# Two layers of directional convolution scans: contiguous map rows, column state in small tiles, lanes 64 steps apart, chains turned over in groups of eight rows

## The chip, the core and the metric

The kernel runs on one core of one Trainium2 chip. The metric is the device time of one launch in microseconds (us). The core has five engines that run side by side and wait for each other by semaphores: PE (TensorE, matrix products), DVE (VectorE), ACT (ScalarE), POOL (GpSimd) and SP (SyncE), which here issues nearly all DMAs between HBM and SBUF. Every engine works through its own instructions strictly in order.

## What is computed

Input `x` is float32 [32 batches, 48 channels, 64 rows h, 128 columns w]. Two layers follow each other, each `x = x + scan(groupnorm(x))`, where the group norm has 16 groups per batch and the scan is four recurrences, each started from the result of the one before:

```python
nxt = inp + conv1d(carry, w, b)        # 5 taps, 48 x 48 channels, across the other axis
D = scan(down_w, rows 0..63)           # each row from the row above, conv along w
U = scan(down_w, rows of D, bottom up) # conv along w
R = scan(right_w, columns of U)        # each column from the one to its left, conv along h
L = scan(left_w, columns of R, right to left)
```

So a layer is 63 + 63 dependent row steps and 127 + 127 dependent column steps, and nothing of one batch's step can start before its previous step has ended. The parallelism is over batches.

## The kernel before

Channels of even and odd positions along the convolved axis lie side by side on the partitions (0 to 47 and 64 to 111, the `SIDES`; P = 112), so one step (`step`) is three accumulated 112 x 112 products into one PSUM tile (with the pair of positions before, the pair itself, the pair after), and one DVE instruction `scalar_tensor_tensor` (below: the update, L180) that adds PSUM, bias and the input and writes the new state. Each float32 product shows as two PE records, so a step is six records.

Four batches make a chain (G = 4), so a row step (`d`, `u` in the names) works on 4 x 64 = 256 columns of the moving operand and a column step (`r`, `l`) on 4 x 32 = 128. Two chains are in flight, one per lane. `run_lane` is a Python generator that yields after each step, and the driver calls the two lanes in turn: step n of lane 0, step n of lane 1, and so on. Both lanes are always at the same step of the same scan. A list scheduler then sets the final order of each engine.

The map of a lane lies in SBUF as [batch][pair of w][r][pair of h], that is `[P, G, WP, 2, HP]`. A column `col(v)` is 32 adjacent words per batch; a row `row(h)` is 64 words that lie 64 words (256 bytes) apart. The down scan runs in place on rows; the up scan writes its state to small contiguous tiles `carry` (two per lane), from which `place` (two ACT copies per step, L188) puts each row where the right and left scans read it; these two run in place on columns.

Between two scans stands a chain change. Whole batches move: `load_x` brings one batch in two DMAs of 768 KB, `add_scan` adds the map to it (POOL, L106), `store_x` writes it to `mid` (the layer 0 result in HBM) or `out`, `stats` takes its norm (8 `bn_stats` on DVE, a small matmul, a chain of one-column instructions), and `normalize` writes it into the map (half on ACT L152, half on POOL L159). Each lane has NX = 2 tiles for this. A chain goes through both layers before the next one starts, so there are 4 pairs of chains x 2 layers = 8 rounds.

## Time and profile before

| | us |
|---|---|
| three runs | 8436.22, 8440.92, 8441.28 (median 8440.92) |
| span of the profiled execution | 8440.7 |
| PE, DVE, ACT, POOL busy | 6745.4, 3721.4, 1902.0, 1264.6 |
| DMA by SP | 251.68 MB |

The span, from the first to the last instruction, is within 1 us of the median run, so rows of the profile can be set against the time directly. Busy times overlap and are not shares of a sum. PE's busy time contains products that take longer than their number of columns asks for, so it has to be read by stage.

### The profile page before, as it was taken

The page shows a single profiled execution, that of the slowest core. Times are in us where ns is not written, and L with a number is a line of the kernel's source. Part 1 is how long each engine was busy: PE and PEld are TensorE (multiplying, and loading weights), DVE is VectorE, ACT ScalarE, POOL GpSimd, SP SyncE. Part 2 cuts the span into 40 slices and gives each one's busy share as a digit, 9 for nine tenths or more (in the row PEclk, how much of TensorE's full clock was granted, in tenths as well). Part 3 has the DMA queues.
Part 4 walks back from the last instruction along what each step waited for, and adds up shares of the span by engine and source line. Part 5 has one row for each costly group of instructions (what it writes and reads, how often), then busy time and mean ns, then how long its engine had stood idle before and what let it go on. Part 6 is the DMA issues. An engine that isn't in the chain of part 4 may idle for free. (4 is left out here: it accounts for less than half of the span.)

```text
span 8440.7 us, 85243 instructions
## 1 busy us (share of the span) xinstructions
PE 6745.4 (80%) x36736; PEld 5026.5 (60%) x36736; DVE 3721.4 (44%) x7235; ACT 1902.0 (23%) x2241; POOL 1264.6 (15%) x199
## 2 busy tenths in 40 slices
PE   4999559994499955999449995599944999559993
PEld 2479524894247952489424795248942479524893
DVE  5345533553334553355333455335532345533552
ACT  3070110700207011070020701107012070110700
POOL 4000330003300033000330003300043000330004
PEclk9999779997699977999769997799976999779997
DMA  9000240005700024000570002400057000340005
GB/s 94 0 1 1 44 76 0 1 1 74 105 0 1 1 41 79 0 1 1 75 105 0 1 1 46 74 0 1 1 75 105 0 1 1 46 74 0 1 1 90
DMA packets 497403, 258.09 MB, mean 31 GB/s; under 512 B 5392, under 2 KB 496912, under 8 KB 497024
## 3 DMA queue, kind: packets, MB, share of 16 engines
q1 hardware_dynamic: 496640, 251.68, 20.7%
q8 instruction: 287, 4.70, 0.2%
q10 hardware_dynamic: 384, 0.96, 0.0%
q14 instruction: 92, 0.75, 0.0%
HBM read 151.95 MB, written 100.66 MB: 30 GB/s over the span
## 5 line engine op out<-in xcount | busy, mean ns | idle before, releaser
L106 POOL TENSOR_TENSOR x<-x,map 112x4096 f32<-112x4096 f32 x64 | 694.3, 10866 | 6611.4 <-issue 3290.5
L123 PE MATMUL ps_stat_x<-mv_x,mask_sb 112*112 112x1 f32 x64 | 16.4, 326 | 728.1 <-DVE mv_x L121 722.2
L188 ACT COPY map<-last 48x256 f32<-48x256 f32 x32 | 21.9, 683 | 2469.5 <-DVE last L180 2469.2
L123 PEld LDWEIGHTS ps_stat_x<-mv_x,mask_sb 112*112 112x112 f32 x64 | 14.9, 286 | 731.8 <-DVE mv_x L121 724.8
L135 ACT ACTIVATE std_m<-var_m 112x1 f32<-112x1 f32 x32 | 6.5, 203 | 1850.4 <-DVE var_m L132 1850.3
L123 PE MATMUL ps_stat_m<-mv_m,mask_sb 112*112 112x1 f32 x64 | 16.4, 326 | 473.8 <-DVE mv_m L121 448.6
L119 DVE BATCH_NORM_STATS2 st_x<-x 112x6 f32<-112x512 f32 x256 | 155.6, 679 | 513.9 <-DMA x<-in_x 513.7
L135 ACT ACTIVATE std_x<-var_x 112x1 f32<-112x1 f32 x32 | 6.5, 203 | 1615.1 <-DVE var_x L132 1615.1
L159 POOL TENSOR_SCALAR map<-x,scale_x,offset_x 48x2048 f32<-48x2048 f32 x64 | 277.8, 4341 | 346.3 <-DVE offset_x L145 340.3
L119 DVE BATCH_NORM_STATS2 st_m<-x 112x6 f32<-112x512 f32 x256 | 160.5, 679 | 340.7 <-POOL x L106 340.7
L159 POOL TENSOR_SCALAR map<-x,scale_m,offset_m 48x2048 f32<-48x2048 f32 x64 | 271.6, 4244 | 195.4 <-DVE offset_m L145 171.3
L123 PEld LDWEIGHTS ps_stat_m<-mv_m,mask_sb 112*112 112x112 f32 x64 | 14.9, 286 | 477.7 <-DVE mv_m L121 450.7
L152 ACT ACTIVATE map<-x,offset_x,scale_x 48x2048 f32<-48x2048 f32 x64 | 279.3, 4364 | 44.9 <-DVE offset_x L145 41.3
L152 ACT ACTIVATE map<-x,offset_m,scale_m 48x2048 f32<-48x2048 f32 x64 | 273.1, 4268 | 51.6 <-DVE offset_m L145 34.1
L130 PE MATMUL ps_stat_m<-sq_m,mask_sb 112*112 112x1 f32 x64 | 16.5, 328 | 151.9 <-DVE sq_m L129 151.9
L180 DVE SCALAR_TENSOR_TENSOR map<-ps_1L1d,b_sb,map 112x256 f32<-112x256 f32 x62 | 75.3, 1215 | 123.7 <-PE ps_1L1d L177 117.9
L180 DVE SCALAR_TENSOR_TENSOR map<-ps_3L1d,b_sb,map 112x256 f32<-112x256 f32 x62 | 75.5, 1217 | 123.1 <-PE ps_3L1d L177 118.0
L180 DVE SCALAR_TENSOR_TENSOR map<-ps_7L0d,b_sb,map 112x256 f32<-112x256 f32 x62 | 76.3, 1231 | 121.2 <-PE ps_7L0d L177 115.6
L180 DVE SCALAR_TENSOR_TENSOR map<-ps_7L1d,b_sb,map 112x256 f32<-112x256 f32 x62 | 75.5, 1217 | 123.0 <-PE ps_7L1d L177 117.9
L180 DVE SCALAR_TENSOR_TENSOR map<-ps_5L1d,b_sb,map 112x256 f32<-112x256 f32 x62 | 75.4, 1216 | 123.0 <-PE ps_5L1d L177 117.9
L180 DVE SCALAR_TENSOR_TENSOR map<-ps_3L0d,b_sb,map 112x256 f32<-112x256 f32 x62 | 76.4, 1232 | 120.7 <-PE ps_3L0d L177 115.4
L180 DVE SCALAR_TENSOR_TENSOR map<-ps_5L0d,b_sb,map 112x256 f32<-112x256 f32 x62 | 76.3, 1231 | 120.6 <-PE ps_5L0d L177 115.5
(617 smaller groups left out, 19622.9 us busy)
## 6 DMA issues: line engine op xcount, KB each, us to landing
x<-in_x SPq DMA_DIRECT2D x128, 768.0 KB, 16.3
mid<-x SPq DMA_DIRECT2D x64, 768.0 KB, 12.1
x<-mid SPq DMA_DIRECT2D x64, 768.0 KB, 16.0
out<-x SPq DMA_DIRECT2D x64, 768.0 KB, 12.6
w_sb<-in_w ACTq DMA_DIRECT2D x1, 882.0 KB, 12.2
mask_sb<-in_mask ACTq DMA_DIRECT2D x1, 49.0 KB, 1.9
b_sb<-in_b ACTq DMA_DIRECT2D x1, 2.6 KB, 5.4
```

What stands on the lines that cost most here:

```text
L106: nc.gpsimd.tensor_tensor(xt, xt, maps[lane][:, j].rearrange("c p r q -> c q (p r)"), ALU.add)
L119: nc.vector.bn_stats(st[:, s, :], flat[:, bass.ts(s, SEG)])
L123: nc.tensor.matmul(ps[:, 0:1], mask_sb, mv[:, 0:1], start=True, stop=True)
L130: nc.tensor.matmul(ps[:, 1:2], mask_sb, sq, start=True, stop=True)
L135: nc.scalar.activation(std, var, AF.Sqrt)
L152: nc.scalar.activation(maps[lane][SIDES[0], j, :, hs, :], view[hsl, :, 0, :], AF.Identity, bias=offset[hsl], scale=scale[hsl],)
L159: nc.gpsimd.tensor_scalar(maps[lane][SIDES[1], j, :, hs, :], view[hsl, :, 1, :], scale[hsl], offset[hsl], ALU.mult, ALU.add,)
L180: nc.vector.scalar_tensor_tensor(dst, ps, b_sb[:, layer, way : way + 1], inp, ALU.add, ALU.add)
L188: nc.scalar.copy(maps[lane][SIDES[hs], :, :, ws, q], carry[SIDES[ws]])
```

## The change

What it does, by parts:

- **Map layout.** The map becomes [batch][pair of h][r][pair of w], `[P, G, HP, 2, WP]`. Now `row(h)` is 64 adjacent words per batch, and `col(v)` is 32 words that lie 128 words (512 bytes) apart.
- **Column state.** The right and left scans no longer run in place. Each step writes a small contiguous tile `cur` (six per lane), the next step's products read that tile, and a POOL `tensor_copy` puts it into the map.
- **Lanes 64 steps apart.** Lane 0 starts 64 steps ahead of lane 1 (OFFSET). A lane also walks all its layer 0 chains first and then all its layer 1 chains.
- **Turn-over in groups.** The chain change is cut into NG = 8 groups of four row pairs (eight rows) of all four batches. Six tiles (`ring`) are shared by both lanes. For each group `turn_over` adds the old chain's map to its `x` rows (`turn_rows`, four POOL adds of 112 x 512), stores them, takes `bn_stats` for the next layer, and normalizes the new chain's rows into the same map rows (`normalize_rows`, 16 instructions of 48 x 256, on ACT, for the first group half on DVE). Groups 0 and 1 are turned over before the new down scan starts and group 2 ahead of its first step, one further group every eight steps. Each group takes eight load DMAs for the old rows, eight for the new, eight stores, of 96 KB each.
- **Statistics of x** come from a separate pass over `x` (`batch_stats`, `plan_stats`), spread over steps of the chain before by `spare()`; scales and offsets are kept for all chains.

```diff
-        cpool.tile([P, G, WP, 2, HP], F32, tag=f"map{i}", name=f"map{i}")
+        cpool.tile([P, G, HP, 2, WP], F32, tag=f"map{i}", name=f"map{i}")
...
+    def load_rows(src: bass.AP, chain: int, g: int) -> bass.AP:
+        t = free.pop(0)
+        for j in range(G):
+            for side in range(2):
+                nc.sync.dma_start(t[SIDES[side], j], rows(src, chain, g, j, side))
+        return t
...
+    def turn_rows(lane: int, layer: int, chain: int, g: int, t: bass.AP, st):
+        dst = out if layer else mid
+        for j in range(G):
+            mine = t[:, j].rearrange("c q (p r) -> c q r p", r=2)
+            nc.gpsimd.tensor_tensor(
+                mine, mine, maps[lane][:, j, g * GH : (g + 1) * GH], ALU.add
+            )
+        store_rows(dst, chain, g, t)
+        if st is not None:
+            for j in range(G):
+                nc.vector.bn_stats(st[:, j, g, :], t[:, j].rearrange("c q w -> c (q w)"))
+    def normalize_rows(lane: int, layer: int, chain: int, g: int, t: bass.AP, split: bool):
...
+                    if split and ws:
+                        nc.vector.tensor_scalar(dst, src, s, o, ALU.mult, ALU.add)
+                    else:
+                        nc.scalar.activation(dst, src, AF.Identity, bias=o, scale=s)
...
-            nc.scalar.copy(maps[lane][SIDES[hs], :, :, ws, q], carry[SIDES[ws]])
+            nc.scalar.copy(maps[lane][SIDES[hs], :, q, ws, :], carry[SIDES[ws]])
...
         def row(h):
-            return m[:, :, :, h % 2, h // 2]
+            return m[:, :, h // 2, h % 2, :]
         def col(v):
-            return m[:, :, v // 2, v % 2, :]
+            return m[:, :, :, v % 2, v // 2]
...
+            def turn_over(g, heads=heads, before=before, layer=layer, chain=chain, st=st, src=src):
+                old, new = heads[g]
+                if before is not None:
+                    turn_rows(lane, *before, g, old, st)
+                    free.append(old)
+                normalize_rows(lane, layer, chain, g, new, g == 0)
+                free.append(new)
+                if g + 2 < NG:
+                    load_heads(heads, before, layer, chain, g + 2)
+                if g == NG - 1 and st is not None:
+                    finish_stats(1, before[1], st)
...
+            for g in range(2):
+                turn_over(g)
+            for h in range(1, H):
+                if h % (2 * GH) == 1 and h // (2 * GH) + 2 < NG:
+                    turn_over(h // (2 * GH) + 2)
+                dst = row(h) if h < H - 1 else last
+                step(lane, layer, DOWN, f"{key}d{h}", row(h - 1), row(h), dst)
+                yield
...
+            for v in range(1, W):
+                cur = col_pool.tile([P, G, HP], F32, tag=f"col{lane}", name=f"col_{key}r{v}")
+                step(lane, layer, RIGHT, f"{key}r{v}", prev, col(v), cur)
+                if v < W - 1:
+                    nc.gpsimd.tensor_copy(col(v), cur)
...
+                if v % 3 == 0:
+                    spare()
+                yield
...
+                if v == AHEAD and k + 1 < len(walk):
+                    heads = []
+                    for g in range(2):
+                        load_heads(heads, (layer, chain), *walk[k + 1], g)
...
     lanes = [run_lane(i) for i in range(LANES)]
+    next(lanes[0])
+    for _ in range(OFFSET):
+        next(lanes[0])
```

The order of the engines shows where the work went. In these rows a name such as `ps_0L1d15` is the PSUM tile of chain 0, layer 1, down step 15; the trailing number is a buffer's. First PE inside a down scan, before:

```order
L173 MATMUL ps_0L1d16_5089<-map0_79,w_sb_72 112x256
L174 MATMUL ps_0L1d16_5089<-map0_79,w_sb_72 112x4x63
L177 MATMUL ps_0L1d16_5089<-map0_79,w_sb_72 112x4x63
L173 MATMUL ps_1L1d16_5094<-map1_80,w_sb_72 112x256
L174 MATMUL ps_1L1d16_5094<-map1_80,w_sb_72 112x4x63
```

And PE inside a down scan of lane 0 (chain 2), after:

```order
L222 MATMUL ps_1L0l40_6160<-col_1L0l41_6099,w_sb_75 112x128
L223 MATMUL ps_1L0l40_6160<-col_1L0l41_6099,w_sb_75 112x4x31
L226 MATMUL ps_1L0l40_6160<-col_1L0l41_6099,w_sb_75 112x4x31
L222 MATMUL ps_2L0d21_6058<-map0_80,w_sb_75 112x256
L223 MATMUL ps_2L0d21_6058<-map0_80,w_sb_75 112x4x63
```

A down step of one lane now alternates with a left step of the other, which reads a `col` tile.

Second, POOL around the same chain change of lane 0, before (the adds stand together, nothing else is on POOL during the scans):

```order
L159 TENSOR_SCALAR map1_80<-x1_1_78,scale_x7_405,offset_x7_407 48x64x32 x2
L106 TENSOR_TENSOR x0_0_75<-x0_0_75,map0_79 112x4096
L106 TENSOR_TENSOR x1_0_77<-x1_0_77,map1_80 112x4096
L106 TENSOR_TENSOR x0_1_76<-x0_1_76,map0_79 112x4096
L106 TENSOR_TENSOR x1_1_78<-x1_1_78,map1_80 112x4096
L159 TENSOR_SCALAR map0_79<-x0_0_75,scale_m0_4639,offset_m0_4641 48x64x32 x2
```

POOL at that place after the change, with the last left column of chain 0 first:

```order
L337 COPY map0_80<-col_0L0l0_5563 112x128
L193 TENSOR_TENSOR xt5_89<-xt5_89,map0_80 112x4x2x64
L337 COPY map1_81<-col_1L0l65_5570 112x128
L193 TENSOR_TENSOR xt5_89<-xt5_89,map0_80 112x4x2x64 x3
L193 TENSOR_TENSOR xt1_85<-xt1_85,map0_80 112x4x2x64 x4
L193 TENSOR_TENSOR xt4_88<-xt4_88,map0_80 112x4x2x64 x4
L337 COPY map1_81<-col_1L0l64_5727 112x128
L337 COPY map1_81<-col_1L0l63_5739 112x128
```

Twelve adds (groups 0, 1 and 2) now stand ahead of the other lane's next column copies. Third, DVE at the same chain change, after:

```order
L229 SCALAR_TENSOR_TENSOR col_1L0l61_5763<-ps_1L0l61_5764,b_sb_76,map1_81 112x128
L229 SCALAR_TENSOR_TENSOR col_1L0l60_5775<-ps_1L0l60_5776,b_sb_76,map1_81 112x128
L199 BN_STATS st_m0_5577<-xt5_89 112x6 x4
L212 TENSOR_SCALAR map0_80<-xt2_86,scales_78,offsets_79 48x4x64 x8
L199 BN_STATS st_m0_5577<-xt1_85 112x6 x4
L199 BN_STATS st_m0_5577<-xt4_88 112x6 x4
L229 SCALAR_TENSOR_TENSOR map0_80<-ps_2L0d1_5722,b_sb_76,map0_80 112x4x64
L229 SCALAR_TENSOR_TENSOR col_1L0l59_5787<-ps_1L0l59_5788,b_sb_76,map1_81 112x128
```

Before, DVE had all 8 `bn_stats` of one batch in a row here, after the last left step of both lanes:

```order
L180 SCALAR_TENSOR_TENSOR map0_79<-ps_0L0l0_4593,b_sb_73,map0_79 112x4x32
L180 SCALAR_TENSOR_TENSOR map1_80<-ps_1L0l0_4598,b_sb_73,map1_80 112x4x32
L119 BN_STATS st_m0_4609<-x0_0_75 112x6 x8
L119 BN_STATS st_m4_4649<-x1_0_77 112x6
L121 BN_AGGR mv_m0_4618<-st_m0_4609 112x2
```

After the change the statistics of three groups and eight normalizing instructions stand ahead of the first update of the new down scan (`ps_2L0d1`), behind five steps that the other lane takes alone.

## Rows read from the trace of the kernel before

**Rows 1.** The page: PE's busy time, and its granted clock in 40 slices.
```profile
PE 6745.4 (80%) x36736; PEld 5026.5 (60%) x36736; DVE 3721.4 (44%) x7235; ACT 1902.0 (23%) x2241; POOL 1264.6 (15%) x199
PEclk9999779997699977999769997799976999779997
```

**Rows 2.** Windows of 50 us: busy by engine, clock, DMA share, GB/s.
```profile
0.00:50.00 50.00, 1.60 (x6) 1.34 (x6) 34.22 (x32) 5.16 (x3) 24.44 (x8) 1.00 1.19 123
...
250.00:300.00 50.00, 50.00 (x118) 22.59 (x117) 20.30 (x20) 0.00 (x0) 0.00 (x0) 1.00 0.00 0
...
500.00:550.00 50.00, 50.00 (x232) 40.07 (x231) 26.42 (x39) 48.65 (x76) 0.00 (x0) 1.00 0.00 1
...
700.00:750.00 50.00, 50.00 (x451) 50.00 (x450) 26.21 (x75) 0.00 (x0) 0.00 (x0) 1.00 0.01 1
...
1050.00:1100.00 50.00, 2.14 (x8) 1.79 (x8) 13.20 (x34) 11.39 (x5) 32.74 (x5) 0.50 0.84 145
```

**Rows 3.** Timeline of an up step: start, length, instruction, idle time before it.
```profile
602.01 0.69 PE L173 MATMUL ps_0L0u<-carry_0L0u,w_sb 112*112 112x256 f32 x2
...
602.96 0.59 PE L177 MATMUL ps_0L0u<-carry_0L0u,w_sb 112*112 112x252 f32 x2
...
614.89 0.48 DVE L180 SCALAR_TENSOR_TENSOR carry_0L0u<-ps_0L0u,b_sb,last 112x256 f32<-112x256 f32 x1 [0.64 <-ACT map L188]
```

**Rows 4.** Timeline of a right step of lane 0.
```profile
701.04 0.44 PE L173 MATMUL ps_0L0r<-map,w_sb 112*112 112x128 f32 x2
...
701.52 0.38 PE L177 MATMUL ps_0L0r<-map,w_sb 112*112 112x124 f32 x2
...
701.93 0.35 DVE L180 SCALAR_TENSOR_TENSOR map<-ps_0L0r,b_sb,map 112x128 f32<-112x128 f32 x1 [0.35 <-PE ps_0L0r L177]
```

**Rows 5.** Groups of updates on DVE: busy, mean ns, idle before.
```profile
L180 DVE SCALAR_TENSOR_TENSOR carry_1L0u<-ps_1L0u,b_sb,map 112x256 f32<-112x256 f32 x62 | 43.1, 696 | 39.2 <-ACT map L188 22.4 <-PE ps_1L0u L177 16.8
...
L180 DVE SCALAR_TENSOR_TENSOR map<-ps_1L1d,b_sb,map 112x256 f32<-112x256 f32 x62 | 75.3, 1215 | 123.7 <-PE ps_1L1d L177 117.9
```

**Rows 6.** Groups of POOL instructions.
```profile
L106 POOL TENSOR_TENSOR x<-x,map 112x4096 f32<-112x4096 f32 x64 | 694.3, 10866 | 6611.4 <-issue 3290.5 <-DVE map L180 3281.1 <-DMA x<-mid 38.6
...
L305 POOL MEMSET const-float32-1.0<- 128x1 f32 x1 | 0.1, 109 | 0.0
```

**Rows 7.** Timeline of PE at the first right steps after a pause.
```profile
619.37 0.77 PE L173 MATMUL ps_0L0r<-map,w_sb 112*112 112x128 f32 x2 [3.53 <-ACT map L188]
...
625.14 0.38 PE L177 MATMUL ps_0L0r<-map,w_sb 112*112 112x124 f32 x2
```

**Rows 8.** SP's issues of `x` loads: count, min/median/max ns.
```profile
L98 SPq DMA_DIRECT2D x<-in_x x128: 558/4299/7077, 0.7 to 7391.4; - x128
```

**Rows 9.** Groups of statistics on DVE and of `place` copies on ACT.
```profile
L119 DVE BATCH_NORM_STATS2 st_m<-x 112x6 f32<-112x512 f32 x256 | 160.5, 679 | 340.7 <-POOL x L106 340.7
...
L188 ACT COPY map<-carry_0L0u 48x256 f32<-48x256 f32 x126 | 82.2, 653 | 2.3
```

**Rows 10.** Timeline of the first chain change.
```profile
962.47 43.28 POOL L106 TENSOR_TENSOR x<-x,map 112x4096 f32<-112x4096 f32 x4 [822.34 <-issue]
...
986.42 8.53 DVE L127 TENSOR_TENSOR dev_m<-mv_m,mean_m 112x1 f32<-112x1 f32 x1
...
1154.67 0.38 PE L123 MATMUL ps_stat_m<-mv_m,mask_sb 112*112 112x1 f32 x2
...
1158.19 0.16 DVE L145 SCALAR_TENSOR_TENSOR offset_m<-mean_m,scale_m 112x1 f32<-112x1 f32 x1
...
1158.53 8.81 POOL L159 TENSOR_SCALAR map<-x,scale_m,offset_m 48x2048 f32<-48x2048 f32 x2 [10.46 <-DVE offset_m L145]
...
1161.08 0.85 DVE L180 SCALAR_TENSOR_TENSOR map<-ps_0L1d,b_sb,map 112x256 f32<-112x256 f32 x1 [2.73 <-PE ps_0L1d L177]
```

**Rows 11.** Timeline of ACT at the start.
```profile
46.32 8.09 ACT L152 ACTIVATE map<-x,offset_x,scale_x 48x2048 f32<-48x2048 f32 x2 [4.43 <-DVE offset_x L145]
```

More of the change, by code (lines that the diff above doesn't have):

```diff
@@ L80 @@
     ]
+    ring = [
+        cpool.tile([P, G, GH, W], F32, tag=f"xt{k}", name=f"xt{k}") for k in range(RING)
+    ]
+    free = list(ring)
     mid = dram.tile([B, C, H, W], F32, tag="mid", name="mid")
-    for i, t in enumerate(maps + [xt for lane in xts for xt in lane]):
+    for i, t in enumerate(ring + maps):
         eng = nc.vector if i % 2 else nc.gpsimd
@@ new lines, in rows, with store_rows @@
+    def rows(ap: bass.AP, chain: int, g: int, j: int, side: int) -> bass.AP:
+        view = ap[chain * G + j].rearrange("c (q r) w -> r c q w", r=2)
+        return view[side][:, g * GH : (g + 1) * GH]
+    def load_rows(src: bass.AP, chain: int, g: int) -> bass.AP:
[4 more added lines that the diff above has]
+        return t
+    def store_rows(dst: bass.AP, chain: int, g: int, t: bass.AP):
+        for j in range(G):
+            for side in range(2):
+                nc.sync.dma_start(rows(dst, chain, g, j, side), t[SIDES[side], j])
@@ new lines, in new_stats, with batch_stats, load, piece @@
+    def new_stats(key: str) -> bass.AP:
+        return stat_pool.tile([P, G, NSEG, 6], F32, tag="st", name=f"st_{key}")
+    def batch_stats(src: bass.AP, b: int, st: bass.AP):
+        half = b % G
+        view = src[b].rearrange("c (s k h) w -> s k c (h w)", s=2, k=2)
+        tiles = []
+        def load(k):
+            t = free.pop(0)
+            flat = t.rearrange("c b q w -> c (b q w)")
+            for side in range(2):
+                nc.sync.dma_start(flat[SIDES[side]], view[side, k])
+            tiles.append((t, flat))
+        def piece(k, s):
+            t, flat = tiles[k]
+            nc.vector.bn_stats(st[:, half, k * NSEG // 2 + s, :], flat[:, bass.ts(s, SEG)])
+            if s == NSEG // 2 - 1:
+                free.append(t)
+        for k in range(2):
+            yield 1, lambda k=k: load(k)
+        for k in range(2):
+            for s in range(NSEG // 2):
+                yield 0, lambda k=k, s=s: piece(k, s)
@@ L187, in place, with run_lane, spare @@
         for ws in range(2):
-            nc.scalar.copy(maps[lane][SIDES[hs], :, :, ws, q], carry[SIDES[ws]])
-    def scan(lane: int, layer: int, key: str, early):
+            nc.scalar.copy(maps[lane][SIDES[hs], :, q, ws, :], carry[SIDES[ws]])
+    def run_lane(lane: int):
         m, last = maps[lane], lasts[lane]
+        chains = list(range(lane, NCHAINS, LANES))
+        walk = [(layer, chain) for layer in range(2) for chain in chains]
+        work = deque()
+        def spare():
+            if work and (work[0][0] <= len(free)):
+                work.popleft()[1]()
@@ L194, in row @@
         def row(h):
-            return m[:, :, :, h % 2, h // 2]
+            return m[:, :, h // 2, h % 2, :]
         def col(v):
-            return m[:, :, v // 2, v % 2, :]
-        for h in range(1, H):
-            dst = row(h) if h < H - 1 else last
-            step(lane, layer, DOWN, f"{key}d{h}", row(h - 1), row(h), dst)
-            yield
-        place(lane, H - 1, last)
-        prev = last
-        for h in range(H - 2, -1, -1):
-            carry = carry_pool.tile(
-                [P, G, WP], F32, tag=f"carry{lane}", name=f"carry_{key}u{h}"
-            )
-            inp = row(h - 1) if h else last
-            step(lane, layer, DOWN, f"{key}u{h}", prev, inp, carry)
-            place(lane, h, carry)
-            prev = carry
-            yield
@@ L259 @@
+        for g in range(NG):
+            t = load_rows(mid, before[1], g)
+            turn_rows(lane, *before, g, t, None)
+            free.append(t)
+            yield
     lanes = [run_lane(i) for i in range(LANES)]
+    next(lanes[0])
+    for _ in range(OFFSET):
+        next(lanes[0])
     while lanes:
```

208 lines of the change are left out of this document (101 added, 107 removed).

## The prediction, made before the changed kernel had run

> **What bounds the kernel now.** I read the page first: PE is busy 6745 of 8441 us at a granted clock that is full in most slices and drops at every chain change [rows 1]. That share mixes stages, so I went to windows [rows 2]. One pair of steps (both lanes) is 12 PE records. In the down scan PE is never idle, yet only 118 records fit in 50 us: 5.08 us for a pair of row steps. In the up scan, with the same number of columns and the same clock, 232 records fit: 2.58 us. The difference between the two is what PE reads: down reads rows of the map whose words lie 256 bytes apart, up reads the contiguous `carry`. In right and left 451 records fit: 1.33 us per pair. Around 1050 us, in a chain change, PE works 2 of 50 us at the low clock. So there are three prices per round of 1055 us (8441 / 8): 63 x 5.08 = 320 us of down, 63 x 2.58 = 163 of up, 254 x 1.33 = 338 of right and left, and the remaining 234 us are the chain change.
>
> Then I read what a single lane's step needs, because the change mixes steps of different length. In the up scan the first record starts at 602.01 and the last product ends at 602.96 + 0.59 = 603.55: 1.54 us. An update of 256 columns from contiguous input takes 0.48 us [rows 3]. In the right scan the products take 701.04 to 701.90, 0.86 us, the update starts 0.03 us later and takes 0.35 [rows 4]; since the lane starts again after 1.33 us, the hand back to PE costs 0.09. So 0.86 + 0.03 + 0.35 + 0.09 = 1.33: right and left already sit on the chain of one lane, not on PE's rate.
>
> **The change, part by part.**
>
> *Rows contiguous.* Down steps read what up steps read now, so their products fall to half. A row step alone costs 1.54 + 0.03 + 0.48 + 0.09 = 2.14 us.
>
> *Columns through tiles.* The products still read contiguous words. The update writes contiguous words but reads its input from `col(v)`, 512 bytes apart. The nearest row is the up scan's update: input 256 bytes apart, output contiguous, 696 ns on average [rows 5] against 480 contiguous, 0.216 us for 256 columns, so 0.108 for 128. Bounds: nothing (0.35), and the down scan's worst group, strided on both sides, 1215 ns, which is 0.735 more for 256 and 0.37 for 128. I take 0.108: a lane's column step becomes 1.44 us (1.33 to 1.70).
>
> *The POOL copies.* 4,064 new copies of 112 x 128. No such row exists. The smallest POOL instruction takes 0.109 us, and the slowest rate is the add's, 10,866 / 4096 = 2.65 ns per column [rows 6]; so 0.11 to 0.11 + 128 x 2.65 = 0.45 us. Even two in 1.44 us fit, and the next step waits for the tile, not for the copy. I take them as free; what hides them is that POOL idles in all scans now.
>
> *Lanes 64 apart.* From PE's order of the changed kernel I counted how steps alternate: 976 pairs of a row step with a column step, 467 of two row steps, 1504 of two column steps, and alone 106 row and 80 column steps. A mixed pair has 2.58 / 2 + 1.33 / 2 = 1.96 us of PE work, less than the row step's own chain, so 2.14. Two row steps are PE-bound, 2.58. So 976 x 2.14 + 467 x 2.58 + 1504 x 1.44 + 106 x 2.14 + 80 x 1.44 = 2089 + 1205 + 2166 + 227 + 115 = **5802 us** for all steps.
>
> *The chain change.* What is removed is 8 x 234 us. What replaces it are 14 changes of one lane each. An add of 512 columns is 512 x 2.65 = 1.36 us, so four of a group take 5.4. For a lane whose old chain was in layer 0, the first update of the new down scan stands on DVE behind the statistics of groups 0, 1 and 2. Group 2's old rows are only loaded once group 0's store has been issued, after 0.4 + 5.4 = 5.9 us; 0.79 MB of stores and 0.79 MB of loads at 145 GB/s [rows 2] end about 17 us after the last left step, the adds behind them 22 to 23. Meanwhile the other lane takes five or six left steps, some 7 us. So 16 us are lost in the four such changes of lane 0. In the other ten DVE's order puts only group 0, or 0 and 1, ahead, or nothing but the eight normalizing instructions, and up steps between them: I take 7 us, half of the 12 adds' time less the steps taken. With 4 x 16 + 10 x 7 = 134, and PE running its first products at the low clock for 5.8 us after a pause of 3.5 us (0.77 for the first two records, 0.38 again from 625.14) [rows 7], some 4 us each with the smaller gaps inside the scan: **200 us**.
>
> Later groups are loaded two ahead. SP issues 24 DMAs of 96 KB per group. The median issue of 768 KB takes 4.3 us [rows 8], 0.54 for an eighth, 13 us per group; the data, 2.36 MB, take 16.3 us at 145 GB/s. Eight mixed pairs take 17.1. Both just fit. I put **50 us** for what does not, and for ACT: a `place` copy takes 0.65 [rows 9], and two copies and two normalizing instructions per pair of row steps are up to 2.6 us of 2.58.
>
> *Statistics among the steps.* 352 of the 512 `bn_stats`, 679 ns each [rows 9], now stand between updates. DVE has about a third of that free in a pair, so 0.45 each: **160 us**. Fourteen times the chain from matmul to offset runs in between: 1154.67 to 1158.35, 3.7 us [rows 10]: **50 us**.
>
> *Start and end.* The first offset comes at 46.3 us now, after one batch [rows 11]; all four batches are 6.3 MB, 51 us at 123 GB/s [rows 2], plus the first rows: 60, and 20 for lane 1's start: **80 us**. At the end the last chain's eight groups go load, add, store in SP's order: 8 issues (4.3), some 2 to land, one add, 8 issues: 12 us each, **100 us**. Lane 0's end lies under lane 1's last scan.
>
> *Sum:* 5802 + 200 + 50 + 160 + 50 + 80 + 100 = **6442 us**, against a span of 8440.7 and a median of 8440.9. I predict 6440.
>
> **A rule against the change.** A chain change has POOL adds and DVE work side by side. The trace shows both answers: a one-column DVE subtraction with two SBUF inputs took 8.53 us while a POOL add ran, ending with it (986.42 + 8.53 = 994.95; three adds from 962.47 end at 962.47 + 0.75 x 43.28 = 994.93), while the scan's update, with one input in PSUM, took 0.85 us beside a POOL instruction [rows 10]. So the updates stay free of POOL, and the squares and products of the statistics do not. The Trainium skill, page "SBUF — State Buffer", section "Who interferes with whom", states the same for two SBUF inputs, agrees that one SBUF input is free of it, and adds that a float32 `tensor_scalar` from SBUF to SBUF may take both ports, in which case the second to issue is fully blocked. The new eight normalizing `tensor_scalar` on DVE would be such instructions; no run here shows one.
>
> **The rivals.**
> - *Normalizing on DVE is blocked by the adds* (that rule): each of the eight waits for one add, 8 x 1.36 = 11 us in each of 14 changes, 150 us more: 6590. For it: the 8.53 us. Against: in four changes DVE waits for the adds anyway. Chance 0.15.
> - *The turn-over is bound by its transfers.* Loads alone ran at 123 GB/s at the start [rows 2]; 2.36 MB then take 19.2 us, and if SP stands at each group's store until its adds are done (5.4 us) instead of loading, a group takes 24.6 instead of 17.1: 7.5 x 6 groups x 14 = 630 us: 7070. Against: two groups are in flight. Chance 0.17.
> - *The strided input costs as much as in the down scan*: 1.70 instead of 1.44 in 1504 pairs, 390 us more: 6830. Chance 0.07.
> - *Less is lost*: the input's stride costs nothing (-165) and the other lane covers the changes and statistics to half (-200): 6075. Chance 0.13.
> - *Slower than before: the POOL copy is the bound.* Two copies per pair of column steps; to lose 2000 us, each of 1504 pairs must cost 1.33 us more, 2.77, so a copy must take 1.39 us, three times the upper bound. It decides from there. Chance 0.02.
> - No change: 0.01, the same thing a little weaker.
> - The forecast itself: 0.45, with 6250 to 6580 as its own range.
>
> **How the numbers follow.** 0.2% is about what a measurement here can tell from no change. Below 6050 I leave 0.06, above 7090 about 0.1; the range 6050 to 7090 takes in every case in which the kernel gets faster, without their fringes. Faster 0.97, same 0.01, slower 0.02.
>
> **What would show it.** Down steps: 0.21 us per record instead of 0.43. Mixed pairs at 2.1 us, column pairs at 1.4, with updates of 0.46. POOL copies under 0.45. A gap on PE of 10 to 20 us once per chain and lane, and the clock at the low level only there. The prediction is wrong if column pairs take over 1.6 us (copies or strided input), if PE stands still every eight steps of a down scan (transfers), or if the lanes' waits for each other add gaps to mixed pairs that neither chain has.

## The result, and the profile after

The changed kernel takes 6429.69 us (median of four executions, 6427.40 to 6433.65), the kernel before 8439.43 on the same chip: a ratio of 0.762, 95% interval 0.761 to 0.763. The profiled execution has a span of 6431.9 us. 6440 had been predicted; as the parts below show, errors of 180 us to one side and 189 to the other stand behind the 10 us of difference.

From the page (PE's busy time and its granted clock in 40 slices):

```profile
PE 5963.7 (93%) x36544; PEld 5054.6 (79%) x36544; DVE 3206.9 (50%) x6964; ACT 2010.0 (31%) x3985; POOL 2298.6 (36%) x4584
PEclk9999999999999999999999999999999999999985
```

The page's chain of work that ended last, by engine:

```profile
PE 77%; ACT 7%; issue 4%; DVE 4%; POOL 3%; DMA 2%; SPq 1%; POOLq 0%; DVEq 0%; ACTq 0%
```

Windows of 50 us, in order of time: row pairs, mixed pairs, a chain change, mixed pairs with thirty `bn_stats` among them, column pairs, and lane 1 alone at the end (a column pair is two column steps, one of each lane; a mixed pair is a row step and a column step).

```profile
350.00:400.00 50.00, 50.00 (x235) 41.41 (x235) 30.82 (x63) 16.13 (x40) 0.00 (x0) 1.00 0.51 112
450.00:500.00 50.00, 50.00 (x278) 40.66 (x277) 21.02 (x46) 18.55 (x46) 9.31 (x23) 1.00 0.00 1
850.00:900.00 50.00, 36.79 (x178) 29.13 (x177) 30.25 (x56) 31.69 (x53) 23.65 (x33) 0.78 0.62 149
1200.00:1250.00 50.00, 49.47 (x279) 40.57 (x278) 39.45 (x91) 18.77 (x47) 9.34 (x23) 1.00 0.64 126
1550.00:1600.00 50.00, 50.00 (x405) 47.09 (x404) 29.01 (x68) 0.00 (x0) 27.21 (x68) 1.00 0.00 1
6300.00:6350.00 50.00, 36.54 (x139) 29.46 (x139) 9.74 (x23) 0.00 (x0) 17.27 (x31) 0.50 0.38 85
```

With twelve records to a pair, a pair of row steps, one lane in its down and the other in its up scan, takes 12 x 50 / 235 = 2.55 us (5.08 in down and 2.58 in up before, [rows 2]), a mixed pair 2.16, a pair of column steps 1.48 (1.33 before). The chain change that stood in windows of 2 PE us out of 50 [rows 2] is now a window with 36.8.

Groups of instructions that answer to [rows 5, 6, 9], and the new ones:

```profile
L229 DVE SCALAR_TENSOR_TENSOR col_3L0r<-ps_3L0r,b_sb,map 112x128 f32<-112x128 f32 x127 | 54.7, 431 | 42.6 <-PE ps_3L0r L226 40.2 <-POOL map L325 1.3 <-POOL map L337 0.5
L337 POOL COPY map<-col_6L1l 112x128 f32<-112x128 f32 x127 | 51.6, 406 | 45.9 <-DVE col_6L1l L229 45.9
L193 POOL TENSOR_TENSOR xt<-xt,map 112x512 f32<-112x512 f32 x512 | 653.8, 1303 | 275.6 <-DMA xt<-in_x 134.5 <-DMA xt<-mid 130.4 <-DVE map L229 8.4
L212 DVE TENSOR_SCALAR map<-xt,scales,offsets 48x256 f32<-48x256 f32 x128 | 134.7, 1052 | 13.3 <-POOL xt L193 9.0 <-DVE offsets L185 0.3
L237 ACT COPY map<-carry_0L0u 48x256 f32<-48x256 f32 x126 | 50.7, 403 | 72.4 <-DVE carry_0L0u L229 71.4
```

The update of a column costs 0.43 us (0.35 before), a column copy on POOL 0.41, an add 1.30. POOL waits 265 us for loads over the whole run, and DMA and SP's issues hold 3% of the chain that ended last, start and end included: transfers are not the bound.

A chain change of lane 0, on DVE (start, length, instruction, idle before):

```profile
843.05 0.43 DVE L229 SCALAR_TENSOR_TENSOR col_0L0l<-ps_0L0l,b_sb,map 112x128 f32<-112x128 f32 x1 [0.41 <-PE ps_0L0l L226]
...
852.54 0.43 DVE L229 SCALAR_TENSOR_TENSOR col_1L0l<-ps_1L0l,b_sb,map 112x128 f32<-112x128 f32 x1 [1.76 <-PE ps_1L0l L226]
852.89 2.47 DVE L199 BATCH_NORM_STATS2 st_m<-xt 112x6 f32<-112x512 f32 x4
855.39 6.86 DVE L212 TENSOR_SCALAR map<-xt,scales,offsets 48x256 f32<-48x256 f32 x8
862.28 4.84 DVE L199 BATCH_NORM_STATS2 st_m<-xt 112x6 f32<-112x512 f32 x8
867.03 0.48 DVE L229 SCALAR_TENSOR_TENSOR map<-ps_2L0d,b_sb,map 112x256 f32<-112x256 f32 x1
867.41 0.43 DVE L229 SCALAR_TENSOR_TENSOR col_1L0l<-ps_1L0l,b_sb,map 112x128 f32<-112x128 f32 x1
```

Lane 0's last update of the old chain starts at 843.05, the first of the new one at 867.03. Lane 1 has nothing to do with this change, yet it stands from 852.54 to 867.41 as well: DVE works off statistics, normalizing and statistics in one piece, 14 us, and both lanes' updates are behind it. This is the first of 14 changes, and the three like it are worse: there lane 0's updates stand 21.5 us apart with a single step of lane 1 between them. By the starts of the updates, the gaps of all 14 changes sum to 264 us; the 35 steps of the other lane in them are worth some 63 us at undisturbed prices, so about 200 us are lost. POOL at the time of the first change:

```profile
845.55 13.88 POOL L193 TENSOR_TENSOR xt<-xt,map 112x512 f32<-112x512 f32 x11
```

A step of lane 0 alone, near the start:

```profile
123.31 0.48 DVE L229 SCALAR_TENSOR_TENSOR map<-ps_0L0d,b_sb,map 112x256 f32<-112x256 f32 x1 [2.97 <-PE ps_0L0d L226]
123.85 1.20 PE L222 MATMUL ps_0L0d<-map,w_sb 112*112 112x256 f32 x2 [0.58 <-DVE map L229]
...
126.77 0.48 DVE L229 SCALAR_TENSOR_TENSOR map<-ps_0L0d,b_sb,map 112x256 f32<-112x256 f32 x1 [2.97 <-PE ps_0L0d L226]
```

The same product took 0.69 us in [rows 3]; here it takes 1.20, and a step 3.45 us instead of 2.14.

### The profile page after: what moved, and what is told of

The parts are those of the page before. It is cut to its first block, busy times and chain, and to the rows that moved or that the text cites. A ratio compares the mean times of both kernels' runs of the same rounds, so it can differ in the third digit from the quotient of the medians.

```text
span 6431.9 us, 100151 instructions
## 1 busy us (share of the span) xinstructions
PE 5963.7 (93%) x36544; PEld 5054.6 (79%) x36544; DVE 3206.9 (50%) x6964; ACT 2010.0 (31%) x3985; POOL 2298.6 (36%) x4584
## 4 chain that ended last, share of the span: by engine, by line
PE 77%; ACT 7%; issue 4%; DVE 4%; POOL 3%; DMA 2%; SPq 1%; POOLq 0%; DVEq 0%; ACTq 0%
ACT map L214 6%; POOL xt L193 3%; DMA xt<-in_x 1%; PE ps_7L1l L222 1%; DVE map L212 1%; PE ps_0L0d L222 1%; ACT map L237 1%; DMA xt<-mid 1%; PE ps_4L1l L222 1%; PE ps_7L1u L222 1%; PE ps_1L0u L222 1%; PE ps_1L1u L222 1%; PE ps_3L1u L222 1%; PE ps_7L0u L222 1%; PE ps_5L1u L222 1%
## 5 line engine op out<-in xcount | busy, mean ns | idle before, releaser
L214 ACT ACTIVATE map<-xt,offsets,scales 48x256 f32<-48x256 f32 x1920 | 1182.5, 616 | 1825.1 <-POOL xt L193 1786.9
L193 POOL TENSOR_TENSOR xt<-xt,map 112x512 f32<-112x512 f32 x512 | 653.8, 1303 | 275.6 <-DMA xt<-in_x 134.5
L325 POOL COPY map<-col_0L0r 112x128 f32<-112x128 f32 x126 | 51.0, 405 | 540.4 <-DVE col_0L0r L229 539.9
L199 DVE BATCH_NORM_STATS2 st_m<-xt 112x6 f32<-112x512 f32 x256 | 172.0, 686 | 40.9 <-POOL xt L193 39.2
L139 DVE BATCH_NORM_STATS2 st_x<-xt 112x6 f32<-112x512 f32 x256 | 164.8, 681 | 2.1 <-DMA xt<-in_x 2.0
L325 POOL COPY map<-col_6L0r 112x128 f32<-112x128 f32 x126 | 51.0, 405 | 254.8 <-DVE col_6L0r L229 254.8
L325 POOL COPY map<-col_4L0r 112x128 f32<-112x128 f32 x126 | 51.1, 405 | 254.4 <-DVE col_4L0r L229 250.9
L325 POOL COPY map<-col_0L1r 112x128 f32<-112x128 f32 x126 | 51.0, 405 | 253.3 <-DVE col_0L1r L229 253.3
L212 DVE TENSOR_SCALAR map<-xt,scales,offsets 48x256 f32<-48x256 f32 x128 | 134.7, 1052 | 13.3 <-POOL xt L193 9.0
L325 POOL COPY map<-col_6L1r 112x128 f32<-112x128 f32 x126 | 51.0, 405 | 249.9 <-DVE col_6L1r L229 249.9
L325 POOL COPY map<-col_2L1r 112x128 f32<-112x128 f32 x126 | 51.0, 405 | 248.0 <-DVE col_2L1r L229 248.0
L325 POOL COPY map<-col_2L0r 112x128 f32<-112x128 f32 x126 | 51.1, 405 | 243.9 <-DVE col_2L0r L229 243.8
L325 POOL COPY map<-col_4L1r 112x128 f32<-112x128 f32 x126 | 51.0, 405 | 243.0 <-DVE col_4L1r L229 242.9
L222 PE MATMUL ps_7L1l<-col_7L1l,w_sb 112*112 112x128 f32 x252 | 76.3, 394 | 48.9 <-DVE col_7L1l L229 48.9
```

Of the source, the lines that this page charges most:

```text
L139: nc.vector.bn_stats(st[:, half, k * NSEG // 2 + s, :], flat[:, bass.ts(s, SEG)])
L193: nc.gpsimd.tensor_tensor(mine, mine, maps[lane][:, j, g * GH : (g + 1) * GH], ALU.add)
L199: nc.vector.bn_stats(st[:, j, g, :], t[:, j].rearrange("c q w -> c (q w)"))
L212: nc.vector.tensor_scalar(dst, src, s, o, ALU.mult, ALU.add)
L214: nc.scalar.activation(dst, src, AF.Identity, bias=o, scale=s)
L222: nc.tensor.matmul(ps, wt[:, 1], prev, start=True, stop=False)
```

## The experiments

Times are medians; each ratio is to the kernel before on the same chip. The theory: the gain has two halves, TensorE's rate on strided rows and the hidden chain change, and what is lost of it lies on the engines beside PE. The rival: only one of the halves counts.

**old_map.** The map as before; all else as changed (`place`, adds and normalizing follow).

```diff
-        cpool.tile([P, G, HP, 2, WP], F32, tag=f"map{i}", name=f"map{i}")
+        cpool.tile([P, G, WP, 2, HP], F32, tag=f"map{i}", name=f"map{i}")
...
-            return m[:, :, h // 2, h % 2, :]
+            return m[:, :, :, h % 2, h // 2]
...
-            return m[:, :, :, v % 2, v // 2]
+            return m[:, :, v // 2, v % 2, :]
```

> The changed kernel with one part undone: the map lies in memory as before (rows strided by 256 bytes, columns contiguous); lag, small column tiles, copies and turn-over stay. Theory: the rate of the products over a strided operand is the largest part of the gain. 1008 down steps then read strided rows again, 1.25 us more each for TensorE alone (half of 5.08 - 2.58), and up to 2.1 us more where the lane's own chain sets the pair (its update at 1.2 instead of 0.48 us as well): 6430 + 1260 to 2100 - 150 (column input contiguous again) = 7540 to 8380 us, middle 7950. Rival: the gain comes from hiding the chain change, and the layout matters little under a lag in which one lane fills the other's gaps: below 6830 us.

Measured: 7684.72 us, ratio 0.912 (0.910 to 0.913), 1255 us slower than the changed kernel. Windows of row pairs and of column pairs:

```profile
450.00:500.00 50.00, 50.00 (x158) 28.78 (x157) 23.66 (x37) 16.08 (x26) 0.00 (x0) 1.00 0.13 36
700.00:750.00 50.00, 49.78 (x426) 47.37 (x425) 24.67 (x71) 0.00 (x0) 20.88 (x71) 1.00 0.00 1
```

A row pair with one strided partner takes 3.80 us instead of 2.55, 1.25 more as half of 5.08 - 2.58, at the same granted clock of 1.00. A column pair takes 1.41 with contiguous input: the strided input costs 0.07 to 0.08, some 120 us over the 1504 pairs, so the 1255 us are what is left after that gain.

**layout_alone.** The kernel before with the new layout, column tiles (two per lane, shared with `carry`) and POOL copies; lanes in step, old chain change.

```diff
...
-            step(lane, layer, RIGHT, f"{key}r{v}", col(v - 1), col(v), col(v))
+            cur = state(lane, HP, f"col_{key}r{v}")
+            step(lane, layer, RIGHT, f"{key}r{v}", prev, col(v), cur)
+            nc.gpsimd.tensor_copy(col(v), cur)
+            prev = cur
```

> The kernel before with one part of the change: contiguous map rows, column states in small tiles, and the copies on GpSimd; lanes in step and the old chain change stay. Theory: row pairs of down fall from 5.08 to 2.58 us (8 x 63 x 2.50 = 1260 less), column pairs rise from 1.33 to 1.48 (2032 x 0.15 = 305 more): 8440 - 1260 + 305 = 7490 us, with 7400 to 7550 since the adds and the normalizing read other strides. So the lag and the turn-over would be worth 1060 us, about as much as the layout alone. Rival: strided columns make the copies or the updates the bound when all 2032 pairs are column pairs of two lanes in step: over 7700.

Measured: 7265.17 us, ratio 0.862 (0.860 to 0.864). 225 us better than expected, and the windows of down and of right and left are as expected:

```profile
200.00:250.00 50.00, 50.00 (x236) 41.43 (x235) 18.86 (x40) 0.00 (x0) 0.00 (x0) 1.00 0.00 1
700.00:750.00 50.00, 49.80 (x402) 46.52 (x401) 28.94 (x67) 0.00 (x0) 27.40 (x67) 1.00 0.01 1
```

The rest is mostly in the chain change, which I had left as it was: its seven pauses sum to 1253 us instead of 1418 by the updates, and the up scans to 1293 instead of 1354. Adds and normalizing in it:

```profile
L106 POOL TENSOR_TENSOR x<-x,map 112x4096 f32<-112x4096 f32 x64 | 575.6, 9006 | 93.6 <-DMA x<-mid 91.6
L159 POOL TENSOR_SCALAR map<-x,scale_m,offset_m 48x2048 f32<-48x2048 f32 x64 | 139.0, 2171 | 202.5 <-DVE offset_m L145 199.6
```

The add falls from 10.87 to 9.01 us [rows 6], the normalizing on POOL from 4.4 (two in 8.81, [rows 10]) to 2.17. So the layout alone is worth 1167 us against the kernel before on the same chip, and lag and turn-over together the other 840 or so; how these divide between the two was not tested.

**no_col_copy.** Leaves out all POOL column copies.

```diff
-                if v < W - 1:
-                    nc.gpsimd.tensor_copy(col(v), cur)
...
-            nc.gpsimd.tensor_copy(col(W - 1), prev)
...
-                nc.gpsimd.tensor_copy(col(v), cur)
```

> The changed kernel without the copies of the column tiles into the map on GpSimd, so that left reads columns that right has not changed, and the adds columns that left has not changed. Theory A: the copies are hidden, and nothing waits for them: 6430 us, within 15. Theory B: the update of a column step now waits for two engines (the product, and the copy that last read its tile), and this second wait is the 0.07 us by which it starts later behind the products than before (0.10 against 0.03): 1504 column pairs x 0.07 = 105 less, about 6325 us, pairs at 1.41 instead of 1.48.

Measured: 6158.11 us, ratio 0.730 (0.729 to 0.732): 272 us less. Column pairs and normalizing:

```profile
1550.00:1600.00 50.00, 50.00 (x424) 47.74 (x424) 30.41 (x71) 0.00 (x0) 0.00 (x0) 1.00 0.00 1
```

```profile
L212 DVE TENSOR_SCALAR map<-xt,scales,offsets 48x256 f32<-48x256 f32 x128 | 48.6, 411 | 3.3 <-DVE offsets L185 0.3
```

Pairs at 1.42 us bear theory B out. But that is only about 105 us; this edit does more than it was made for. Without copies the adds need nothing from right and left and run long before the change, so the end after the last update shrinks from 67.3 us to 1.3, and the normalizing runs with no add beside it at 411 ns instead of 1052. The remaining 100 us are left for the chain changes, whose gaps sum to 74 us instead of 264; what eats up the rest of that gain was not traced. That a copy finishes in time does not make it free, and this run overstates what it costs.

**double_copy.** Each POOL copy of a column issued twice.

```diff
-                    nc.gpsimd.tensor_copy(col(v), cur)
+                    for _ in range(2):
+                        nc.gpsimd.tensor_copy(col(v), cur)
```

> The changed kernel with every column copy on GpSimd made twice. In a pair of column steps GpSimd then has 4 x 0.405 = 1.62 us of copies against a pair of 1.48. Theory: GpSimd becomes the bound of these pairs, at 1.62 to 1.8 us: 1504 x (0.14 to 0.32) = 210 to 480 more, 6640 to 6910 us; mixed pairs (0.81 of 2.15) do not change. Rival: the copies have room enough through the six tiles of each lane, and the time stays below 6460.

Measured: 6441.49 us, ratio 0.764 (0.763 to 0.766), 12 us more. The theory falls. One line of its window shows why:

```profile
1550.00:1600.00 50.00, 50.00 (x409) 47.39 (x407) 29.38 (x68) 0.00 (x0) 45.81 (x137) 1.00 0.01 2
```

137 copies keep POOL busy for 45.8 of 50 us, 0.334 each instead of 0.406 alone: copies that follow each other overlap, and four take 1.34 us of a pair's 1.47. POOL has room for twice the copies and little beyond.

**batch4.** Column state in tiles of four columns, one POOL copy for four.

```diff
-                cur = col_pool.tile([P, G, HP], F32, tag=f"col{lane}", name=f"col_{key}r{v}")
+                if four is None or v % 4 == 0:
+                    four = col_pool.tile([P, 4, G, HP], F32, tag=f"col{lane}", name=f"col_{key}r{v}")
+                cur = four[:, v % 4]
...
-                if v < W - 1:
-                    nc.gpsimd.tensor_copy(col(v), cur)
...
+                elif v % 4 == 3 and v < W - 1:
+                    copy_cols(lane, v - 3, v + 1, four)
```

> The changed kernel with column states in tiles of four columns (two such tiles per lane) and one GpSimd copy for four columns instead of four. Only the first update of four then waits for GpSimd as well. Theory B of the run without copies (the second wait costs 0.07 us of each update): three quarters of 105 us are gained, 6430 - 80 = 6350, column pairs at 1.43. Rival: what the copies cost is the contention of two engines on SBUF, which is the same for the same bytes: 6430 within 15.

Measured: 6364.18 us, ratio 0.754 (0.753 to 0.755): 66 less, and 1.43 us a pair:

```profile
1500.00:1550.00 50.00, 50.00 (x419) 47.82 (x417) 30.34 (x77) 0.20 (x1) 18.81 (x19) 1.00 0.01 1
```

The same bytes are copied (1.09 us for 512 columns), so contention for bytes is out. The trace shows which updates pay. Two updates beside one and the same copy, the fourth column of lane 1's tile and the first of lane 0's next tile, each with the product that it waits for:

```profile
1513.81 0.38 PE L226 MATMUL ps_3L0l<-col_3L0l,w_sb 112*112 112x124 f32 x2
1514.02 1.09 POOL L243 COPY map<-col_2L0l 112x512 f32<-112x512 f32 x1 [3.13 <-DVE col_2L0l L229]
1514.23 0.45 DVE L229 SCALAR_TENSOR_TENSOR col_3L0l<-ps_3L0l,b_sb,map 112x128 f32<-112x128 f32 x1 [0.27 <-PE ps_3L0l L226]
1514.53 0.38 PE L226 MATMUL ps_2L0l<-col_2L0l,w_sb 112*112 112x124 f32 x2
1515.02 0.43 DVE L229 SCALAR_TENSOR_TENSOR col_2L0l<-ps_2L0l,b_sb,map 112x128 f32<-112x128 f32 x1 [0.34 <-PE ps_2L0l L226]
```

The fourth column starts 0.04 us behind its product, the first one 0.11. So it is over the whole run: updates that go on in a tile start 0.04 us behind the product (median), whether POOL is busy or not, and the first update of a tile 0.11. The cost lies on the update that writes a tile again which POOL has copied from, though the copy is long done. That the wait for a second semaphore is what takes the 0.07 us is the likely reason; it was not shown by itself.

**no_split.** The first group normalized on ACT alone.

```diff
-                normalize_rows(lane, layer, chain, g, new, g == 0)
+                normalize_rows(lane, layer, chain, g, new, False)
```

> The changed kernel with all 16 normalizing instructions of a chain's first group on ScalarE, none on VectorE. The run without column copies has shown that the chain changes as a whole cost about 166 us (6430 - 6158 - 105), 12 each. Theory: the eight normalizing instructions on VectorE (1052 ns on average against 411 alone), blocked by the adds on GpSimd, hold up the updates of both lanes, 7 us in each of 14 changes; without them the first step waits for ScalarE, 1.3 + 16 x 0.62 = 11.2 us after the last left step instead of some 8, but the other lane runs on: 30 to 80 us less, 6350 to 6400. Rival: the first step waits for whoever normalizes last, and ScalarE takes longer than VectorE did: 14 x 3 = 40 us more, 6470.

Measured: 6372.67 us, ratio 0.755 (0.754 to 0.756), 57 less: 4 us per change. (The 166 us in this expectation also contain the end of 66.) In the change that answers to the one above, lane 1's updates go on to 859.16 us, with

```profile
859.51 7.23 DVE L199 BATCH_NORM_STATS2 st_m<-xt 112x6 f32<-112x512 f32 x12
```

alone left in one piece.

**one_ahead.** Every group turned over one group later.

```diff
-            for g in range(2):
-                turn_over(g)
+            turn_over(0)
...
-                if h % (2 * GH) == 1 and h // (2 * GH) + 2 < NG:
-                    turn_over(h // (2 * GH) + 2)
+                if h % (2 * GH) == 1 and h // (2 * GH) + 1 < NG:
+                    turn_over(h // (2 * GH) + 1)
```

> The changed kernel with each group of rows turned over one group later: only the first group before the first down step, group 1 at step 1, group 2 at step 9. Theory: what VectorE does for groups 1 and 2 ahead of the first update (eight bn_stats, 4.8 us, in the eight changes whose old chain was in layer 0) and the ScalarE queue of three groups (3 x 9.9 us, in which the other lane's place copies wait, in the seven changes of lane 1) shrink: 8 x 4.8 + 7 x 3 = 60 us less, 6370. Rival: the groups now come too late (adds 5.2, normalizing 9.9, eight pairs 17 us) and PE stops at step 8, 16 and so on: 0 to 50 us more.

Measured: 6324.38 us, ratio 0.749 (0.748 to 0.751), 105 less; PE does not stop for late groups. More was gained than expected, and the changed kernel's trace shows where it had been lost, inside the down scan (ACT, then DVE):

```profile
1035.51 10.14 ACT L214 ACTIVATE map<-xt,offsets,scales 48x256 f32<-48x256 f32 x16
1045.68 3.35 ACT L237 COPY map<-carry_2L0u 48x256 f32<-48x256 f32 x8
```

```profile
1046.54 0.48 DVE L229 SCALAR_TENSOR_TENSOR carry_2L0u<-ps_2L0u,b_sb,map 112x256 f32<-112x256 f32 x1 [2.98 <-ACT map L237]
```

Sixteen normalizing instructions of a group stand in one piece before the `place` copies of the other lane's up scan; its three `carry` tiles (the change adds one to the two before) run full, and the update waits. In this run ACT has them in pieces:

```profile
1036.50 1.88 ACT L214 ACTIVATE map<-xt,offsets,scales 48x256 f32<-48x256 f32 x3
1038.39 0.81 ACT L237 COPY map<-carry_2L0u 48x256 f32<-48x256 f32 x2
```

The row pairs (by the starts of all 6,080 updates) fall from 2.82 us on average to 2.66, while the gaps of the changes stay at 260 us in all.

**late_stats.** As one_ahead, with `bn_stats` given out by the steps.

```diff
-            for j in range(G):
-                nc.vector.bn_stats(st[:, j, g, :], t[:, j].rearrange("c q w -> c (q w)"))
...
+                    for j in range(G):
+                        late.append(lambda j=j: row_stats(j, g, old, st))
...
+                for _ in range(3):
+                    if late:
+                        late.popleft()()
```

> As the run that turns over one group later, and the bn_stats of an old group's rows are given out three per down step instead of four at once ahead of the step. Theory: the serial work on VectorE at the change is the loss, so 2.7 us of bn_stats for group 0 go in eight changes, 22 us less than that run, about 6350; bn_stats between mixed steps cost nearly nothing, as the 0.07 us of those among column pairs let expect. Rival: the statistics between the steps cost what they took before: the same as that run within 10 us.

Measured: 6295.16 us, ratio 0.746 (0.745 to 0.747), 29 less than one_ahead: as the theory had it (22). (The `bn_stats` among column pairs that this expectation names do not exist: none of the changed kernel's stands in a column pair. Among mixed pairs they cost 0.08 us each.)

**fill_solo.** An extra product per step wherever a lane runs alone.

```diff
+    def fill():
+        if alone[0]:
+            nc.tensor.matmul(warm, mask_sb, flat_w[:, 0:256], start=True, stop=True)
```

> The changed kernel, and wherever one lane runs alone (64 steps at the start, 64 at the end) one extra product of 256 columns on constant data, behind each step's products, into a PSUM tile that nobody reads. In the changed kernel a row step alone takes 3.45 us, with products of 1.05 to 1.20 us for two records, and a column step alone 2.18, 0.62 to 0.77 for two, at a granted clock of 0.50 in the windows of the end. Theory: TensorE falls to its lower level because it idles while it waits for the update, and the extra product (0.6 us at the full rate) closes that gap: row steps alone at 2.1 to 2.3, column steps at 1.45 to 1.6: 64 x 1.25 + 64 x 0.65 = 120 less, 6310. Rival: the rate of a lane alone has another cause, and the extra work only delays the next step: 0 to 128 x 0.6 = 77 us more.

Measured: 6384.76, 6387.33 and 6442.46 us, and one execution of 19543 us, at a mean granted clock of 0.289, that nothing here explains and that is left out. (The clocks of the three are 0.964, 0.963 and 0.951, so the third may have had its first steps at the lower level; only the first has a trace.) The experiment did not do what it was made for: the scheduler put all 120 products, which depend on nothing, into one piece ahead of the first step.

```profile
L243 PE MATMUL warm<-w_sb,mask_sb x240: 379/379/737, 15.6 to 70.3; 112*112 112x256 f32 x120
```

The profiled execution (6384.76) ran lane 0's steps alone at 2.1 to 2.2 us from the first one on (but for two), the other kernel with the same piece (best_fill) at 3.45. Windows of both just behind it:

```profile
75.00:100.00 25.00, 18.28 (x72) 11.59 (x72) 5.52 (x12) 24.35 (x41) 0.00 (x0) 1.00 0.26 63
```

```profile
75.00:100.00 25.00, 20.88 (x46) 12.31 (x44) 3.39 (x7) 24.37 (x40) 0.00 (x0) 0.50 0.26 59
```

So the rate of a lane alone is that of TensorE's clock: 72 records in 25 us at a granted 1.00, 46 at 0.50, for the same instructions with the same gap of 0.58 us in each step. Behind the extra products both runs are at the full level; in best_fill, after a pause of PE of 2.00 us and one step, the clock falls in the second step (a first product of 1.06 us at 73.60), in fill_solo, after a pause of 1.86 us, it does not. What decides between the two was not tested. The steps alone at the end ran at 0.50 in all these runs; products spread among them were not tried.

**best.** late_stats and batch4, and the first group's DVE half of the normalizing on POOL.

```diff
-                        nc.vector.tensor_scalar(dst, src, s, o, ALU.mult, ALU.add)
+                        nc.gpsimd.tensor_scalar(dst, src, s, o, ALU.mult, ALU.add)
```

> The late statistics (6295), the tiles of four columns (66 less than the changed kernel), and the half of the first group's normalizing that stood on VectorE on GpSimd, behind the adds there (a quarter of a microsecond each by the 2.17 us of the eight times longer ones in the run with the layout alone; taking it off VectorE gave 57 with ScalarE in its place). Theory: the three parts are separate losses and add up: 6295 - 66 - 40 = 6190 us, 6165 to 6215. Rival: the late statistics have taken most of what blocking cost at the changes, so that the normalizing gives nothing more: 6230.

Measured: 6220.36 us, ratio 0.737 (0.736 to 0.738): 3.3% less than the changed kernel, the fastest here. The gains add up (6295 - 66 = 6229), and moving the normalizing gave at most the 9 us that are left, within the interval of the ratio, as the rival had it; an instruction takes 565 ns on POOL, twice the estimate. **best_fill**, the same with the extra products:

> The kernel with these three parts and the extra products in the steps of one lane alone. Theory: the gain of the extra products is independent of the others, 120: 6070 us. Rival: as in the run with the extra products alone.

Measured: 6235.21 us, ratio 0.738 (0.737 to 0.740): 15 more. The products delay the first step by 17 us, and the clock fell to its lower level in the second step.

**lag127.**

```diff
-OFFSET = 64
+OFFSET = 127
```

> The changed kernel with the lanes 127 steps apart instead of 64, so that no pair of two row steps is left. Pair arithmetic with the measured 2.15 (mixed), 2.55 (two rows) and 1.48 (two columns): a round of 381 steps is 254 x 2.15 + 127 x 1.48 = 734 us against 128 x 2.15 + 63 x 2.55 + 190 x 1.48 = 717, so 17 x 7 = 120 more; and 63 more steps of each lane run alone, at 3.45 and 2.18 us, for 63 pairs of some 2 us that go: 230 more. Theory (a mixed pair costs a row step's own chain, and a lane alone runs at the low rate): 6780 us, 6720 to 6840. Rival: what the lag gains is that rows of one lane lie under columns of the other, and more of it is better: below 6430.

Measured: 6576.06 us, ratio 0.779 (0.777 to 0.780). 146 more than with 64, between theory and rival. The updates of its trace form 1848 mixed, 1012 column and 40 row pairs, 88 row and 192 column steps alone. At the undisturbed prices (2.15, 1.49, 2.56; alone 3.45 for the first 50 rows, 2.13 after, 2.18 for the last 130 columns, 1.49 else) that is 6212 us; the changed kernel's 972, 1508, 473, 98 and 76 give 5981 (66 columns at 2.18). So 231 more in steps instead of 350: the pairs take 36 more (-6 expected: 120 for the rounds less 126 for the pairs that go), columns alone 217 more (137), rows alone 21 less instead of 217 more. The last is what the expectation had wrong: lane 1's first update comes at 235.6 us, at 231.6 in the changed kernel, so the larger lag leaves no further rows alone at the start. The rest is 85 us less, which fits the row pairs that wait for ACT (1332 us in the changed kernel's trace for 473 pairs, 121 more than at 2.56, and only 40 such pairs here).

## Why the prediction came out right

The steps, start and end of the changed kernel, in us (measured: the counts and prices just named, 5981; the first update starts at 57.45, the last at 6364.6; the remainder 6431.9 - 57.5 - 67.3 - 5981):

| term | predicted | measured |
|---|---|---|
| mixed pairs | 976 x 2.14 = 2089 | 972 x 2.15 = 2090 |
| row pairs | 467 x 2.58 = 1205 | 473 x 2.56 = 1211 |
| column pairs | 1504 x 1.44 = 2166 | 1508 x 1.49 = 2247 |
| rows alone | 106 x 2.14 = 227 | 50 x 3.45 + 48 x 2.13 = 275 |
| columns alone | 80 x 1.44 = 115 | 66 x 2.18 + 10 x 1.49 = 159 |
| changes, later groups, statistics | 200 + 50 + 160 + 50 = 460 | 326 |
| start and end | 80 + 100 = 180 | 125 |
| sum | 6442 | 6432 |

- **Rows contiguous**: right, shown by old_map, in the rate and in the whole (1255 us).
- **Mixed pairs at the row step's own chain**: right to 0.03 us (2.11 and 2.17 are the usual values). A row step alone takes the same at the full clock (2.11 to 2.19 in fill_solo), and the pairs stay at 2.17 in no_col_copy, where the column step is 0.07 us shorter: the row step's chain sets them.
- **Columns through tiles** was undersized. The strided input costs 0.08 (0.108 was taken, with 0.37 as the far bound), but the update also starts 0.10 us behind the product instead of 0.03. "I take them as free" of the POOL copies is the step that failed, by 66 to 105 us: what a copy holds up is not the next step but the later update that writes its tile again, as batch4 shows. Its own length, 0.41 us, lay within the bounds, far from the 1.39 of the rival that ends slower.
- **Steps alone** were priced at the full rate; in 50 row and 66 column steps the products ran at half of it. This is 48 + 44 us. The page's clock row shows 9 throughout the start, so it had to be read from the records: 1.20 instead of 0.69. The sign "the clock at the low level only there", that is in the chain changes, was wrong for both ends of the run.
- **Chain changes**: about 200 us were predicted (the parts named, 134 + 14 x 4, make 190) and about 200 are lost, so of the 326 us of this row some 121 are the row pairs that wait for ACT, where 50 had been set for later groups. For lane 0 after layer 0, 16 us were taken; the first such change shows 15 (24 us from update to update, less 9 for six steps of lane 1), the other three 20. Part of the reason was wrong. Group 2's loads held nothing up: in the change shown, eleven adds ran in one piece, 1.26 us each, and all were done at 859.4, 16 us after lane 0's last update and not 22 to 23. What ends last is DVE, with statistics as the prediction said, and with the normalizing that it had only in a rival.
- **That rival** (normalizing on DVE blocked by adds) did occur: 1052 ns against 411 without adds beside it. Only its price was too high, 57 us in no_split against 150: the 106 instructions that run beside an add take 1.18 us on average, 0.77 more than 0.41 and not 1.36, because an instruction waits for what is left of an add; all but a few of them end 0.15 us behind the end of an add. The Trainium skill, page "SBUF — State Buffer", section "Who interferes with whom", says of a DVE instruction that takes both ports and a GpSimd instruction that the second to issue is fully blocked; these ends agree with that.
- **Transfers** as the bound: no. POOL waits 265 us for loads in all, and DMA and SP's issues hold 3% of the chain that ended last (some 190 us, start and end included), where the rival has 630 us more than the forecast.
- **Statistics among the steps** were oversized: of the two windows of mixed pairs above, the one with thirty `bn_stats` has 279 records and the one without 278. By the starts of the updates one costs a mixed pair 0.08 us on average instead of 0.45, and a row pair nothing that can be seen; DVE has idle time in both. In one piece of 4 to 12, at a chain change, they count in full.

The sum was right because 180 us too little in the steps stood against 189 too much in the rest, where the statistics alone had been given 210. The range of the likeliest case, 6250 to 6580, follows from the argument; the last 10 us are chance.

## What to carry to other kernels

Price a step by its own chain, and then price the stretches in which nothing runs beside it by the rate of products that the records show there, not by that of the busy stretches. When a chain's end is hidden under another chain, look at each engine's queue, not only at the path: a piece of statistics or normalizing that stands in one block on DVE or ACT stops the other chain too, and giving it out step by step, or issuing it one group later, was worth 134 us here with the same work done. A copy on an idle engine that nobody waits for can still cost time by the reuse of its tile; fewer, larger copies take most of that back.

## What the runs showed that I had not expected

- The granted-clock row prints 1.00 at the start while products run at half rate (1.20 us for two records of 256 columns against 0.69); where it prints 0.50, at the end, the records agree with it. The first clock event in this trace is a rise to the full level at 230.5 us, where the steps of 3.45 us end; ahead of it the row prints full speed without an event. The Trainium skill, page "TensorE: Matmul & The Clock Gate", section "Seeing it yourself", warns that clock events of a trace have been seen to be unreliable; here the events that there are agree with the records, and only the stretch ahead of the first one misleads.
- One stream of instructions, with 0.58 us of idle time in each step, holds either level for over 100 us: 2.11 us per step in fill_solo, 3.45 in best_fill.
- The order of the map's words slows every engine that has to stride by it: on POOL an add, which reads the map, went from 10.87 to 9.01 us and `tensor_scalar`, which reads `x` in the map's order, from 4.4 to 2.17; an ACT `place` copy, which writes the map, went from 653 ns [rows 9] to 403.
